# Masking attention scores in a state-space and feed-forward kernel: a select on GpSimd for one key block, four square matmul tiles for the other

## The chip, the core and the metric

The kernel runs on one core of a Trainium2 chip. A core has five engines with a queue of instructions each, worked off in order: TensorE (PE in the profile, its weight loads are PEld), VectorE (DVE), ScalarE (ACT), GpSimd (POOL) and SyncE (SP), which here only issues DMAs. Engines wait for one another by semaphores. TensorE writes its results to PSUM, eight banks of 128 partitions by 512 f32 numbers; the other tensors lie in SBUF.

The metric is the device time of the whole kernel in microseconds (us). The changed kernel is compared with the kernel before on the same chip.

## What is computed

32 sequences of 256 positions with 256 features go through a gated state-space layer, then through two transformer layers with local attention, and the input is added at the end. What the change touches is the local attention. The reference, cut to it:

```python
def local_attention(q, k, v):
    b, h, n, d = q.shape                  # n = 256 positions, 8 heads, d = 64
    w = n // WINDOW                       # WINDOW = 128: two windows
    bq = q.reshape(b, h, w, WINDOW, d) * QK_SCALE
    ...
    bk, bv = (look_around(bk), look_around(bv))   # the window before, and the own one
    ...
    sim = jnp.einsum('bhwid,bhwjd->bhwij', bq, bk)
    i = bt[:, :, None]
    j = btk[:, None, :]
    mask = (i < j) | (i > j + WINDOW) | (j == -1)
    sim = jnp.where(mask, -jnp.finfo(sim.dtype).max, sim)
    attn = jax.nn.softmax(sim, axis=-1)
    out = jnp.einsum('bhwij,bhwjd->bhwid', attn, bv)
    return out.reshape(b, h, n, d)

x = x + _L0_ffn_ref(_L0_cond_ref(x, cond_2048, ...), ...)
```

A query at position i sees the keys from i - 128 to i. With keys in two blocks of 128: the first block's keys are seen by queries of both windows (256 columns, of which a band is masked at either end), the second block's keys only by queries of the second window (128 columns, a triangle of which is masked).

## The kernel before

Sequences are worked in 4 groups of 8 (`NG`, `GB`). Two kinds of work run beside each other. The scan of the state-space layer takes a group at a time through 256 positions: for every position a row is loaded over 128 partitions (`xrep`, L675), scaled on ScalarE (L696), added with a clip on VectorE (`step`, L706, the tile `h`) and read out by TensorE (`read_out`, L718, the tile `y`). GpSimd takes part with the convolution's first tap (`acc`, L477) and the norms (L555, L576, L577).

Beside it run the two attention and feed-forward layers for the group whose scan is done. There are 64 pieces of this, one for each sequence and layer; the code calls the pair of group and layer `Attention(g, l)` and lists the pieces in `seqs`. Each piece is cut into stages, `ST = 8` per piece, and consecutive pieces overlap: `stage(n, i, what)` puts `what` into stage 8n + i, and the main loop calls all that stands in a stage, then lets the scan advance by its share. Within this order a scheduler may still move instructions past each other on an engine; what is wrapped in `tc.keep_in_program_order` stays where it is. The last group's pieces (`apart` is true) run when no scan is left.

`attend` sets the stages of a piece's attention: `project` makes queries, keys and values from the residual (L973) and rotates queries and keys (`rotated`: ScalarE L986, VectorE L989, L994, L999, L1003, GpSimd L997, L1005, L1006), `turn` transposes them (L1012) so that features lie on partitions, two heads above each other: head r of a pair on partitions 64r to 64r + 63.

`scores(b, kw, i0, n)` then works on key block `kw` (0 or 1) and `n` pairs of heads from `i0`. The result `sc` has keys on partitions and queries on columns, one bank per r, each with n parts of `nq` columns: 256 for the first block, 128 for the second. So the first block takes two calls with n = 2, the second one call with n = 4. Where `apart` is false, TensorE first writes the mask into the bank: a matmul of the identity with `mask_t` in bf16 (L1175), 0 where a key is seen and -32768 where it isn't. The score matmuls (L1182) add to that. Both operands have 64 partitions, so that two of them, one per r, fit above each other into the array (64*128 in the profile's rows). ScalarE takes the exponential into `pT` (L1191); -32768 becomes 0.

Where `apart` is true, there is no mask on TensorE: `start` is set on each score matmul, and `mask` (L1203) multiplies the exponentials by `mask_1` of 0 and 1, on GpSimd for the second key block and on VectorE for the first.

`sums` (stage 7) adds the exponentials over the keys on TensorE, four heads side by side as column tiles of 32 (L1212, 128*32 in the rows), and inverts the sum on VectorE (L1220). `values` (stage 7) multiplies with the values in two column tiles of 64 (L1231). The rest of the piece are the division (L1255), the output projection (L1023) and the feed-forward part: `normalise` with `rstd` (L1287), `apply` (L1295), `spread` (L1307), `widen` (L1335, `pa`), `product` (L1353, `ag`) and `narrow` (L1362, `po_f`).

All of PSUM is one pool of eight banks (`ps_w`), and `pT` has six buffers.

Of the kernel before, what the change touches and what calls it, by code (L numbers as in the profile page):

```python
# [14 lines left out]
ALU = mybir.AluOpType  # L15
# [23 lines left out]
W = 128  # L39
# [13 lines left out]
def bc(ap, axis, n):  # L53

    ap = ap.unsqueeze(axis)
    shape = list(ap.shape)
    shape[axis] = n
    return ap.broadcast_to(shape)
# [15 lines left out]
def kernel(  # L74
# [29 lines left out]
    nc = tc.nc  # L104
# [58 lines left out]
    for j in range(NJ):  # L163
# [18 lines left out]
        out=mask_t[:, 0:W], in_=mask_t[:, 0:W], compare_op=ALU.is_ge, fill=MASKED_LOW,  # L182
        base=0, pattern=[[1, W]], channel_multiplier=-1,
    )
    nc.gpsimd.affine_select(
        out=mask_t[:, W : 2 * W], in_=mask_t[:, W : 2 * W], compare_op=ALU.is_ge,
        fill=MASKED_LOW, base=0, pattern=[[-1, W]], channel_multiplier=1,
    )

    mask_1 = const.tile([P, 2 * W], BF, tag="mask_1", name="mask_1")  # L190
# [31 lines left out]
    def program(ctx, exact):  # L222
# [810 lines left out]
        if exact:  # L1033

            mask = rpool.tile([P, 2 * W], FP, tag="mask", name="mask")
            nc.gpsimd.memset(mask, 0.0)
            nc.gpsimd.affine_select(
                out=mask[:, 0:W], in_=mask[:, 0:W], compare_op=ALU.is_ge, fill=MASKED,
                base=0, pattern=[[1, W]], channel_multiplier=-1,
            )  # L1040
            nc.gpsimd.affine_select(
                out=mask[:, W : 2 * W], in_=mask[:, W : 2 * W], compare_op=ALU.is_ge, fill=MASKED,
                base=0, pattern=[[-1, W]], channel_multiplier=1,
            )
# [93 lines left out]
        class Attention:  # L1138
# [27 lines left out]
            def scores(self, b, kw, i0, n):  # L1166


                qT, kT, _ = self.qkv[b]
                nq = S - kw * W  # L1170
                banks = []
                for r in range(2):
                    sc = ps_w.tile([P, n, nq], FP, tag="w", name="sc")
                    if not self.apart:
                        nc.tensor.matmul(  # L1175
                            sc, ident_b, bc(mask_t[:, 0:nq], 1, n), start=True, stop=False
                        )
                    banks.append(sc)
                for i in range(n):
                    for r in range(2):  # L1180
                        rows = slice(r * DH, (r + 1) * DH)
                        nc.tensor.matmul(  # L1182
                            banks[r][:, i, :],
                            kT[rows, i0 + i, kw * W : (kw + 1) * W],
                            qT[rows, i0 + i, kw * W :],
                            start=self.apart,
                            stop=self.apart or i == n - 1,
                        )
                for r in range(2):
                    p = aw.tile([P, n, nq], FP, tag="pT", name="pT", bufs=6)  # L1190
                    nc.scalar.activation(p, banks[r], AF.Exp)  # L1191
                    self.ps[kw, i0, r] = p
                    for i in range(n):
                        self.p[b, kw, i0 + i, r] = p[:, i, :]

            def mask(self, kw, i0):

                e = nc.gpsimd if kw else nc.vector
                for r in range(2):
                    p = self.ps.pop((kw, i0, r))  # L1200
                    n, nq = p.shape[1:]
                    tc.keep_in_program_order(
                        e.tensor_mul(p, p, bc(mask_1[:, 0:nq], 1, n))  # L1203
                    )

            def sums(self, b):

# [207 lines left out]
        def stage(n, i, what, *args):  # L1415
            stages.setdefault(ST * n + i, []).append(partial(what, *args))

        def attend(n, at, b, nxt):

            stage(n, 0, at.turn, b, 1)  # L1420
            stage(n, 3, at.scores, b, 0, 0, 2)
            stage(n, 2, at.scores, b, 1, 0, HEADS // 2)
            stage(n, 5, at.scores, b, 0, 2, 2)
            if at.apart:
                for i, what in ((3, (1, 0)), (4, (0, 0)), (6, (0, 2))):
                    stage(n, i, at.mask, *what)
            stage(n, 7, at.sums, b)
            stage(n, 7, at.values, b)
            stage(n + 1, 0, at.put_inverse)
            stage(n + 1, 2, at.load_inverse)  # L1430
            stage(n + 1, 4, at.divide, b)
            stage(n + 1, 6, at.finish, b)
            if nxt is not None:
                for w in range(NW):
                    for i, a in ((0, 2), (1, 0), (1, 1)):
                        stage(n, 3 * w + i, nxt[0].project, nxt[1], w, a)
                stage(n, 6, nxt[0].turn, nxt[1], 0)
# [27 lines left out]
        for n, (g, l, b) in enumerate(seqs):  # L1465
            nxt = (ats[n + 1], seqs[n + 1][2]) if n + 1 < len(seqs) else None
            attend(n, ats[n], b, nxt)
            feed(n, g, l, b)
# [24 lines left out]
        for t in range(max(stages) + 1):  # L1493
# [3 lines left out]
            g, r = divmod(t + 1 + group - reload, group)  # L1497
# [124 lines left out]
```

## Time and profile before

| | us |
|---|---|
| median of 3 runs (3637.0 to 3640.93) | 3637.98 |
| the profiled execution's own time | 3633.24 |
| its span, first to last instruction | 3631.4 |
| busy in the span: TensorE | 3511.0 |
| VectorE | 2684.7 |
| ScalarE | 2160.2 |
| GpSimd | 1816.2 |
| L1175, mask matmuls: 288, busy | 88.1 |
| L1182, score matmuls of 256 columns: 1024 records, busy | 145.2 |
| L1182, score matmuls of 128 columns: 1024 records, busy | 74.4 |

The granted clock of TensorE was 0.990 over the span. The durations are those of the one profiled execution. A matmul with f32 operands stands twice in the records, so 1024 records are 512 matmuls. The row of a group gives the busy time of all its instructions together, with overlaps counted once, and then the mean duration of one; since matmuls overlap, the two differ.

The page's view in 40 slices shows how busy each engine is along the span, in tenths:

```profile
PE   7999989999999999999999999999999999999999
DVE  5888889878887877877787878777877545555553
ACT  3566656666666666666666666666666444544443
POOL 4433456545555455545555556455544454544551
```

In the first 5 or 6 slices the scan of the first group runs alone. From there to slice 32 scan and layers run beside each other; the last slices are the last group's layers.

### The profile page before, as it was taken

How to read it: one execution, taken by the hardware profiler on the slowest of the kernel's cores; microseconds unless marked ns; L12 is line 12 of the kernel's file. 1: busy time of each engine (PE TensorE's matmuls, PEld its weight loads, DVE VectorE, ACT ScalarE, POOL GpSimd, SP SyncE). 2: the span in 40 equal slices, each digit the busy share in tenths (PEclk: the TensorE clock that was granted, in tenths of full speed). 3: DMA queues.
4: the chain of work that ended last, by engine and by line, in shares of the span. 5: the costliest groups of instructions: out<-in, count | busy, mean ns of one | idle time of the engine just before them, and what ended most of it. 6: DMA issues, size and time to landing. Idle time of an engine off the chain costs nothing.

```text
span 3631.4 us, 56312 instructions
## 1 busy us (share of the span) xinstructions
PE 3511.0 (97%) x19548; PEld 2271.0 (63%) x19548; DVE 2684.7 (74%) x5113; ACT 2160.2 (59%) x3689; POOL 1816.2 (50%) x1746
## 2 busy tenths in 40 slices
PE   7999989999999999999999999999999999999999
PEld 4444335666666666666666666666666677777677
DVE  5888889878887877877787878777877545555553
ACT  3566656666666666666666666666666444544443
POOL 4433456545555455545555556455544454544551
PEclk9999999999999999999999999999999999999999
DMA  7877665545554555444454555534454112011111
GB/s 196 210 203 207 184 174 144 133 114 135 133 138 127 148 143 145 132 118 123 117 141 125 134 150 138 139 105 129 114 140 119 52 44 66 12 30 33 37 27 37
DMA packets 468763, 435.59 MB, mean 120 GB/s; under 512 B 228724, under 2 KB 308085, under 8 KB 468341
## 3 DMA queue, kind: packets, MB, share of 16 engines
q1 hardware_dynamic: 384018, 419.88, 42.5%
q10 hardware_dynamic: 84450, 12.01, 2.1%
q8 instruction: 158, 2.59, 0.3%
q14 instruction: 137, 1.11, 0.1%
HBM read 383.54 MB, written 46.66 MB: 118 GB/s over the span
## 4 chain that ended last, share of the span: by engine, by line
PE 62%; DVE 18%; DMA 7%; POOL 6%; ACT 4%; issue 3%; SPq 0%; ACTq 0%; DVEq 0%; POOLq 0%
PE ps_qkv L973 13%; PE pa L1335 12%; DVE h L706 7%; PE po_f L1362 7%; PE y L718 4%; DMA xrep<-xnd 4%; PE ps_wo L1023 4%; PE sc L1182 4%; PE ov L1231 3%; DVE acc L488 2%; PE ps_out L796 2%; PE tr_qk L1012 2%; PE ps_in L398 2%; ACT xrep L696 2%; PE rs L1212 2%
## 5 line engine op out<-in xcount | busy, mean ns | idle before, releaser
L706 DVE CUSTOM_DVE_ANT_0 h<-h,xrep,lim 128x512 f32<-128x512 f32 x1024 | 950.8, 928 | 226.5 <-ACT xrep L696 193.6
L696 ACT ACTIVATE xrep<-xrep,beta 128x512 f32<-128x512 f32 x960 | 673.2, 719 | 356.6 <-DMA xrep<-xnd 258.0
L973 PE MATMUL ps_qkv<-qkv,res 128*128 128x512 f32 x1536 | 715.0, 600 | 21.0 <-DVE ag L1353 9.7
L1335 PE MATMUL pa<-hT,w 128*128 128x256 f32 (+1 forms) x2816 | 679.9, 383 | 1.6 <-ACT hT L1313 0.9
L1335 PEld LDWEIGHTS pa<-hT,w 128*128 128x128 f32 (+1 forms) x2816 | 514.9, 188 | 147.5 <-issue 55.7
L997 POOL TENSOR_TENSOR rot<-rot,swp 128x512 f32<-128x512 f32 x256 | 336.1, 1313 | 441.3 <-DVE swp L994 330.8
L973 PEld LDWEIGHTS ps_qkv<-qkv,res 128*128 128x128 f32 x1536 | 280.1, 190 | 310.4 <-issue 239.7
L1005 POOL TENSOR_TENSOR rn<-ss,neg_half 128x8 f32<-128x8 f32 x256 | 459.3, 1794 | 18.0 <-DVE ss L1003 8.0
L718 PE MATMUL y<-h,ly 128*32 128x512 f32 x2048 | 361.7, 615 | 11.7 <-DVE h L706 9.3
L1287 POOL TENSOR_TENSOR rstd<-ve,neg_half 128x2 f32<-128x2 f32 x64 | 46.3, 723 | 609.6 <-DVE ve L1285 592.1
L1362 PE MATMUL po_f<-ag,w 128*128 128x256 f32 x1280 | 307.4, 387 | 5.1 <-DVE fo L1373 5.1
L1006 POOL TENSOR_TENSOR rot<-rot,rn 128x512 f32<-128x512 f32 x256 | 292.4, 1142 | 20.1
L1353 DVE SCALAR_TENSOR_TENSOR ag<-pa,b_sb,ag 128x256 f32<-128x256 f32 x320 | 152.7, 477 | 197.7 <-ACT ag L1346 197.3
L1362 PEld LDWEIGHTS po_f<-ag,w 128*128 128x128 f32 x1280 | 236.1, 191 | 69.4 <-issue 11.9
L986 ACT ACTIVATE sq<-ps_qkv 128x512 f32<-128x512 f32 x256 | 151.8, 595 | 208.3 <-PE ps_qkv L973 148.7
L1346 ACT ACTIVATE ag<-pa,b_sb 128x256 f32<-128x256 f32 x320 | 150.1, 469 | 177.3 <-PE pa L1335 175.2
L488 DVE SCALAR_TENSOR_TENSOR acc<-xr,wc_sb,acc 128x256 f32<-128x256 f32 x384 | 192.5, 526 | 56.7 <-POOL acc L477 55.4
L1023 PE MATMUL ps_wo<-oT,wo 128*128 128x256 f32 x1024 | 231.7, 379 | 1.4 <-ACT ag L1346 1.4
L989 DVE TENSOR_TENSOR rot<-ps_qkv,rc_sb 128x512 f32<-128x512 f32 x256 | 175.3, 685 | 75.8 <-ACT sq L986 75.7
L1182 PE MATMUL sc<-qT,kT 64*128 64x128 f32 (+1 forms) x2048 | 219.6, 343 | 0.0
L1191 ACT ACTIVATE pT<-sc 128x512 f32<-128x512 f32 x384 | 208.4, 596 | 12.6 <-PE sc L1182 10.5
L1023 PEld LDWEIGHTS ps_wo<-oT,wo 128*128 128x128 f32 x1024 | 194.3, 190 | 29.3 <-ACT ag L1346 2.2
(157 smaller groups left out, 5653.3 us busy)
## 6 DMA issues: line engine op xcount, KB each, us to landing
xrep<-xnd SPq DMA_DIRECT2D x960, 256.0 KB
rb<-inv SPq DMA_DIRECT2D x128, 256.0 KB
xnd<-xn SPq DMA_DIRECT2D x64, 256.0 KB
qkv<-in_wqkv_dram SPq DMA_DIRECT2D x24, 512.0 KB
ahead<-xs_a SPq DMA_DIRECT2D x48, 256.0 KB
xp<-ahead SPq DMA_DIRECT2D x48, 256.0 KB
xd<-xnd SPq DMA_DIRECT2D x192, 64.0 KB
w<-in_w_dram SPq DMA_DIRECT2D x80, 128.0 KB
```

The lines of the kernel that those rows point to most:

```text
L488: nc.vector.scalar_tensor_tensor(acc, xr[:, :, k : k + CH], wc_sb[:, ch, k : k + 1], acc, ALU.mult, ALU.add,)
L696: scaled = nc.scalar.activation(bx, ck[c].pop(("bx", t), bx), AF.Copy, scale=ck[c]["beta"][:, t : t + 1])
L706: nc.vector._custom_dve(TENSOR_ADD_SAT, out=h_new, in0=state["h"], in1=bx, s0=ck[c]["lim"][:, 0, t : t + 1], s1=ck[c]["lim"][:, 1, t : t + 1],
L718: nc.tensor.matmul(ck[c]["y", hb][32 * q : 32 * q + 32, :], ly[hb % 2][:, 32 * t : 32 * t + 32], ck[c].pop(("h", hb * TB + t)), start=(i = ...
L973: nc.tensor.matmul(ps, res[b][:, k, t0 : t0 + W], wt["qkv", a][:, k], start=(k == 0), stop=(k == KM - 1),)
L997: nc.gpsimd.tensor_add(rot, rot, swp)
L1005: nc.gpsimd.tensor_tensor(rn, ss, neg_half, ALU.pow)
L1006: nc.gpsimd.tensor_mul(rot, rot, bc(rn, 2, DH))
L1023: nc.tensor.matmul(po[:, d], wt["wo", 0][:, c, d * P : (d + 1) * P], oT[:, c, :], start=(c == 0), stop=(c == NC_ - 1),)
L1182: nc.tensor.matmul(banks[r][:, i, :], kT[rows, i0 + i, kw * W : (kw + 1) * W], qT[rows, i0 + i, kw * W :], start=self.apart, stop=self.apa ...
L1335: nc.tensor.matmul(dst[x], wt["w1", m][:, k, x], self.h[:, k], start=(k == 0), stop=(k == KM - 1),)
L1362: nc.tensor.matmul(self.po[:, d], wt["w2", 0][:, m, d * P : (d + 1) * P], self.ag[m], start=(m == 0), stop=(m == len(MCH) - 1),)
```

## The change

In the second key block (`kw` = 1) of all groups TensorE writes no mask any more. The exponentials of all entries are taken, and `mask` then runs in every piece: GpSimd's `affine_select` goes over `pT` and writes 0 wherever the column (the query) is less than the partition (the key). It reads one tensor, where the multiplication that the last group had before read two. `mask` for the second key block now stands in stage 3 for all pieces, one stage after its scores.

In the first key block of the groups 0 to 2 the mask matmuls stay. The score matmuls are cut in two by keys: keys 0 to 63 with the queries 0 to 191, keys 64 to 127 with the queries 64 to 255. Each is 64 partitions by 64 columns of weights and 192 columns long, and with two heads they lie on four square tiles of the array (row half by r, column half by keys). The queries left out for either half are masked for all of its keys, and hold what the mask matmul wrote.

The last group's first key block is as before, on VectorE.

```diff
@@ scores
                 nq = S - kw * W
+                masked = kw == 0 and not self.apart
+                nm = 2 if masked else 1
+                mk = W // nm
                 banks = []
                 for r in range(2):
                     sc = ps_w.tile([P, n, nq], FP, tag="w", name="sc")
-                    if not self.apart:
+                    if masked:
                         nc.tensor.matmul(
                             sc, ident_b, bc(mask_t[:, 0:nq], 1, n), start=True, stop=False
                         )
...
-                        nc.tensor.matmul(
-                            banks[r][:, i, :],
-                            kT[rows, i0 + i, kw * W : (kw + 1) * W],
-                            qT[rows, i0 + i, kw * W :],
-                            start=self.apart,
-                            stop=self.apart or i == n - 1,
-                        )
+                        for m in range(nm):
+
+                            k0 = m * mk
+                            q0, q1 = (k0, k0 + W + mk) if masked else (0, nq)
+                            nc.tensor.matmul(
+                                banks[r][k0 : k0 + mk, i, q0:q1],
+                                kT[rows, i0 + i, kw * W + k0 : kw * W + k0 + mk],
+                                qT[rows, i0 + i, kw * W + q0 : kw * W + q1],
+                                start=not masked,
+                                stop=not masked or i == n - 1,
+                            )
@@ mask
-                e = nc.gpsimd if kw else nc.vector
                 for r in range(2):
                     p = self.ps.pop((kw, i0, r))
                     n, nq = p.shape[1:]
-                    tc.keep_in_program_order(
-                        e.tensor_mul(p, p, bc(mask_1[:, 0:nq], 1, n))
-                    )
+                    if kw:
+                        masked = nc.gpsimd.affine_select(
+                            out=p, in_=p, compare_op=ALU.is_ge, fill=0.0, base=0,
+                            pattern=[[0, n], [1, W]], channel_multiplier=-1,
+                        )
+                    else:
+                        masked = nc.vector.tensor_mul(p, p, bc(mask_1[:, 0:nq], 1, n))
+                    tc.keep_in_program_order(masked)
@@ attend
             stage(n, 5, at.scores, b, 0, 2, 2)
+            stage(n, 3, at.mask, 1, 0)
             if at.apart:
-                for i, what in ((3, (1, 0)), (4, (0, 0)), (6, (0, 2))):
+                for i, what in ((4, (0, 0)), (6, (0, 2))):
                     stage(n, i, at.mask, *what)
```

## The prediction

> **What bounds the kernel now.** I read the page's busy shares first, then busy time by stage, then the chain of waits, then the rows of the instructions that change, and last the timeline of single score calls.
>
> The page's first part, and two stretches of the view of busy time by stage (each engine's busy us, with the count of its instructions):
>
> ```profile
> PE 3511.0 (97%) x19548; PEld 2271.0 (63%) x19548; DVE 2684.7 (74%) x5113; ACT 2160.2 (59%) x3689; POOL 1816.2 (50%) x1746
> ...
> 527.00:2960.00 2433.00, 2380.52 (x13842) 1561.02 (x13842) 1908.11 (x3599) 1544.17 (x2637) 1284.25 (x1192) 1.00 0.47 126
> 2960.00:3631.00 671.00, 663.55 (x3852) 480.62 (x3852) 346.01 (x689) 311.12 (x492) 305.23 (x244) 1.00 0.13 35
> ```
>
> TensorE leads in both. The stretch 527 to 2960 us holds the 48 sequences of the first three groups, whose scores get their mask from TensorE; there TensorE is busy 97.8%, VectorE 78%, GpSimd 53%. The last stretch holds the 16 sequences of the last group (`apart`). One sequence of the first kind takes 2433 / 48 = 50.7 us.
>
> Busy 97.8% doesn't mean that each us taken from TensorE is a us off the time. So next the chain of waits, first over the whole span, by engine, and then by line for 527 to 2960 us:
>
> ```profile
> PE 62%; DVE 18%; DMA 7%; POOL 6%; ACT 4%; issue 3%; SPq 0%; ACTq 0%; DVEq 0%; POOLq 0%
> ...
> by line: PE ps_qkv L973 11.9%; PE pa L1335 10.9%; DVE h L706 7.2%; PE po_f L1362 5.9%; PE y L718 4.2%; DMA xrep<-xnd 4.0%; PE ps_wo L1023 4.0%; PE sc L1182 3.6%; PE ps_out L796 3.2%; issue 3.2%; DVE acc L488 3.1%; PE ov L1231 3.1%; POOL rn
> ```
>
> TensorE holds 62% of the chain, not 97%. In between the chain leaves TensorE for VectorE's scan steps (`h`, L706), the loads of `xrep`, and GpSimd; TensorE works there too, but a shorter TensorE stretch only makes it wait sooner. The score matmuls (L1182) hold 3.6% of 2433 us = 88 us of the chain; their busy time in that stretch is 164.7 us by the same view of stages taken for that line. So about 53% of a saving in the scores is on the path.
>
> **What the Trainium skill says.** "Trainium Kernel Development and Optimization", section Quick Reference, calls matmul busy time a bad metric since matmuls are pipelined. The trace agrees: a mask matmul lasts 380 ns in its row, but its successor starts 0.21 us after it (below). "TensorEngine Tiling (Array Packing)", section Key Properties, says that tiles work in parallel and that a change of the tiling mode drains the engine; both can be seen below. "TensorE: Matmul & The Clock Gate", section Measured speedup vs the span model, has 16 tiles by row and column at 10.6 times; the trace of before shows row halves (L1182) and column tiles (L1212, L1231) side by side, but never both at once. "GPSIMD Engine Reference", section Engine selection, says that two-input work is about twice as slow on GpSimd as on VectorE and one-input work is near line rate; the trace agrees in kind (rows below).
>
> The timeline of TensorE around one score call of the first key block, with the second mask matmul from a narrower window, and the rows of what is exchanged (mean ns after the busy us):
>
> ```profile
> 1429.17 0.59 PE L1175 MATMUL sc<-mask_t,ident_b 128*128 128x512 bf16 x2
> ...
> 1429.38 0.38 PE L1175 MATMUL sc<-mask_t,ident_b 128*128 128x512 bf16 x1
> ...
> 1429.69 1.13 PE L1182 MATMUL sc<-qT,kT 64*128 64x256 f32 x8
> 1430.76 1.06 PE L718 MATMUL y<-h,ly 128*32 128x512 f32 x8
> ...
> L1203 POOL TENSOR_TENSOR pT<-pT,mask 128x512 f32<-128x512 f32 x32 | 36.3, 1155 | 1.8 <-ACT pT L1191 1.8
> L290 POOL COPY wide<-wx_sb 128x512 f32<-128x512 f32 x3 | 2.0, 674 | 0.0
> L185 POOL TENSOR_SCALAR_AFFINE_SELECT mask_t<-mask_t 128x128 bf16<-128x128 bf16 x1 | 0.3, 292 | 0.0
> ```
>
> Read the starts. First mask to second: 0.21 us for 512 bf16 columns. Second mask to first score: 0.31, so some 0.10 goes to the change from the full array to row halves. Eight score records (each f32 matmul is recorded twice) take 1.07 us from 1429.69 to 1430.76. They go in pairs, one per row half, and the start of the second pair is 0.32 after the first, the third and fourth 0.21 to 0.22 after the one before: a pair of 256 columns streams in 0.215 us, and the first also shows 0.10 of weight load that nothing hides. The rest to `y` is the drain.
>
> **The change part by part.**
> *Second key block, groups 0 to 2.* Two mask matmuls per sequence go, 48 x 2 = 96. The mode change before the scores stays, since what stands ahead is mostly full array work. So 96 x 0.215 = 21 us of TensorE work. Ends: 0.19 per pair if the change cost grew, 0.52 if the mode change went too; 9 to 25 us.
> *First key block, groups 0 to 2.* Two calls per sequence, 96 in all. The mask matmuls stay. Of 4 matmuls of 256 columns on two row halves become 8 of 192 columns on four square tiles; the 64 columns left out are fully masked ones, and they keep the large negative value that the mask matmul put there. If four tiles run at once, a step costs 0.215 x 192/256 = 0.16 us and the call has four steps as before: 4 x 0.215 + 0.10 = 0.96 before, 4 x 0.16 + 0.05 = 0.69 after. (The 0.05 is my estimate for the unhidden load of 64 weights, half of that of 128.) 0.27 x 96 = 26 us. If the column halves don't overlap: 8 steps of 0.16 + 0.05 = 1.33, or +0.37 x 96 = +36 us. I take the first: the denominator row `rs` (L1212) runs four column tiles so, 32 records in 1.44 us from start to start of the next line on the timeline.
> *Sum on TensorE:* 21 + 26 = 47 us of work less. The order of TensorE's instructions shows few other moves (about 400 lines of 7800 differ, most of them these), and changes of tiling mode fall from 1196 to 1182. On the path 53% of 47: 25 us.
> *GpSimd.* 96 new selects in groups 0 to 2, and in the last group 32 selects in place of 32 multiplications at 1155 ns. A select of 512 f32 elements isn't in the trace. From below, the one-input copy of that size, 674 ns; from above, four times the 128-element select, 4 x 292 = 1168. I take 0.9, since the fixed part of a short one counts four times in the upper end. New work 96 x 0.9 = 86 us in a stretch where GpSimd has 1149 us idle. The select waits for ScalarE's exponentials, and as GpSimd works in order, what stands behind it waits too: by the order, mostly the rotation (L997, L1005, L1006), also `acc` (L477) and `xn` (L576). VectorE waits for `acc` and for `rstd`, TensorE's transposes for `rot`. GpSimd has 6% of the chain, 218 of its 1816 busy us or 12%; at that share the selects cost 86 x 0.12 = 10 us. Ends: 0, as it sits in idle time, and 86 x 0.38 = 33, if every select delays it in the 38% of the time in which the chain is off TensorE.
> The sums of the exponentials come at stage 7, the select at stage 3, so 4/8 of 50.7 us lie between: no wait there. VectorE and ScalarE keep their work; a two-input step `h` may be held up by GpSimd's reads (its durations run from 707 to 1866 ns); with one input to read I take nothing for it, up to 10 us.
> *Last group.* TensorE is 98.9% busy there and its work is the same; GpSimd's 32 x 0.25 = 8 us less is hidden by TensorE: 0.
> *Sum:* 25 - 10 = 15 us off. Against the profiled execution's 3633.2 (span 3631.4 and 1.8 around it): 3618. The median of the runs shown lies 4.8 above that: 3623.
>
> **Rivals.**
> *All of TensorE's saving counts.* For it: 97.8% busy, and its named waits in that stretch are small (the largest, for a free bank after L1353, 10.3 us in all). Against: the chain has 38% elsewhere. 47 less some 5 for GpSimd: 3596.
> *The saving is hidden.* What is taken from TensorE comes back as waits for `h` and `xrep`, because VectorE's bursts set the pace of each sequence, and the path share at the margin falls quickly. About 25 x 0.4 - 10 = 0: 3638, give or take 7.
> *Slower: GpSimd's queue.* A select that is issued before its exponentials are done stands at the head of the queue and holds up `rn` and `rot` of the next sequence's keys, and `acc` of the scan. It decides when a pair of selects costs the path over 25 / 48 = 0.5 us per sequence; with the upper end of 33 and 3 for waits at the head it's 36 - 25 = 11 us: 3649. For it: GpSimd's `rn`, `rot` and `acc` are on the chain. Against: its longest waits are idle time before `rstd` and L997.
> *The tiles don't do what they say* (column halves in turn): TensorE +36 - 21 = +15, of it 53% = 8, and 10 for GpSimd: 3656. Against: the column tiles of L1212.
>
> **How the numbers follow.** Forecast 0.46 (its own range 3610 to 3633), full saving 0.20, hidden 0.16, GpSimd's queue 0.14, tiles in turn 0.04. No change means within 0.2%, 7.3 us, about what a measurement of this kernel can tell. Faster: 0.20 and nearly all of 0.46, 0.63; the same: 0.16 and 0.03; slower: 0.18. The range goes down to the full saving with its upper ends, 3592, and up to where half of the slower cases lie, 3647.
>
> **What would show it.** Mask matmuls 192 instead of 288; score records of 64 x 192 that start in fours some 7 ns apart, fours 0.16 us apart, and a call of 0.8 us; a select row of 0.7 to 1.2 us, x128. Idle time of TensorE in the first three groups up from 52 us to some 85 (47 us of work less, 15 us of time), and their stretch some 15 us shorter, the last group's 671 us the same. Fours further apart than 0.2 us would speak for the tiles in turn; waits of `rn`, `acc` or `rot` behind the select on the chain for GpSimd's queue. I am wrong if the share of the scores on the chain isn't what a saving there is worth.

## The result and the profile after

The changed kernel takes 3622.39 us (median of 5 runs, 3616.12 to 3624.52), the kernel before 3637.98 beside it: the medians are 16 us apart, and the ratio is 0.995, with a 95% interval of 0.9936 to 0.9963. Measured once more beside other kernels it had 0.9961 (0.9953 to 0.9969, from 17 runs). The two ratios are 18 and 14 us less; below, the gain is taken as 14 to 18 us. The forecast was 3623.

First the page's busy shares, its chain by engine, and busy time by stage for the first three groups and for the last, of the changed kernel:

```profile
PE 3476.2 (96%) x20220; PEld 2251.9 (62%) x20220; DVE 2687.0 (74%) x5113; ACT 2157.7 (60%) x3689; POOL 1897.4 (52%) x1842
...
PE 58%; DVE 20%; POOL 7%; DMA 6%; ACT 5%; issue 3%; SPq 0%; ACTq 0%; DVEq 0%; POOLq 0%
...
527.00:2945.00 2418.00, 2339.48 (x14459) 1536.01 (x14459) 1915.18 (x3598) 1542.48 (x2638) 1379.20 (x1287) 0.99 0.48 127
2945.00:3622.00 677.00, 670.02 (x3912) 485.84 (x3910) 342.02 (x692) 313.14 (x496) 290.75 (x246) 1.00 0.13 35
```

TensorE's share of the chain falls from 62% to 58%, VectorE's and GpSimd's rise: what was taken from TensorE isn't all on the path. TensorE idles 2418 - 2339 = 79 us in the first stretch, 52 before. GpSimd has 81 us more to do.

The instructions that changed, from the groups by form, and TensorE's timeline around one score call of the first key block:

```profile
L1209 POOL TENSOR_SCALAR_AFFINE_SELECT pT<-pT 128x512 f32<-128x512 f32 x128 | 99.2, 791 | 1.8 <-ACT pT L1198 1.8
L1189 PE MATMUL sc<-qT,kT 64*64 64x192 f32 x1536 | 87.3, 342 | 0.0
...
L1178 PE MATMUL sc<-mask_t,ident_b 128*128 128x512 bf16 x192 | 59.7, 381 | 20.3 <-DVE ag L1364 19.5 <-DVE zT L787 0.4 <-DVE swp L994 0.4
```

```profile
1415.93 0.59 PE L1178 MATMUL sc<-mask_t,ident_b 128*128 128x512 bf16 x2
1416.45 0.88 PE L1189 MATMUL sc<-qT,kT 64*64 64x192 f32 x16
1417.27 0.70 PE L973 MATMUL ps_qkv<-qkv,res 128*128 128x512 f32 x1
```

From start to start the call takes 1417.27 - 1416.45 = 0.82 us, where it took 1.07. The single records in the trace start in fours, 6 to 7 ns apart, and the fours are 0.21, 0.16 and 0.16 us apart. One pass of 192 columns takes 0.16 us, and four matmuls start within 20 ns: so four square tiles do run at once. The select lasts 0.79 us on average (median 0.64), and GpSimd stood still for its exponentials only 1.8 us in all: it isn't issued too early.

Where along the span the gain comes can be read off the start of the first denominator matmul (`rs`) of each piece in the records. In us, against before; piece 48 is the first of the last group. Each row is one execution, and "again" is a second one of the changed kernel, so differences of some 5 us are scatter: up to piece 0 nearly the same work runs in all of them, and still that column goes from -6.5 to +3.4:

```
piece              0      8     16     24     32     40     48     60
before, us     553.1  963.5 1390.2 1803.9 2218.7 2632.6 2997.7 3468.8
after           -1.4   -0.1   +1.1   +0.8   +2.0   -2.4   -8.5   -8.5
after, again    -2.4   -1.1   -2.3   -3.9   -2.5   -7.3  -13.5  -13.5
tiles only      -1.4   -2.1   -4.6   -6.1   -5.7   -9.8  -13.3  -13.3
no select       -6.5   -7.3  -12.3  -19.3  -25.3  -32.5  -39.4  -39.4
select twice    +3.4   +9.1  +13.1  +13.9  +20.8  +19.2  +14.0  +14.0
```

From piece 48 on nothing changes, as forecast: TensorE paces the last group and has the same work. But the changed kernel gains next to nothing in its first 32 pieces. (The profiled execution is the slowest of the five; its total is 9 us less.) This didn't look like a gain that is spread evenly. It raised a second theory, the scan theory: that a us of TensorE is worth nothing while the scan runs beside it, and all of it once the scan thins out. The path-share theory below is the prediction's: a us of TensorE is worth 0.53 everywhere in groups 0 to 2.

### The profile page after: what moved, and what is told of

It is laid out like the page before. It is cut to its first block, busy times and chain, and to the rows that moved or that the text cites. A ratio compares the mean times of both kernels' runs of the same rounds, so it can differ in the third digit from the quotient of the medians.

```text
span 3622.8 us, 57709 instructions
## 1 busy us (share of the span) xinstructions
PE 3476.2 (96%) x20220; PEld 2251.9 (62%) x20220; DVE 2687.0 (74%) x5113; ACT 2157.7 (60%) x3689; POOL 1897.4 (52%) x1842
## 4 chain that ended last, share of the span: by engine, by line
PE 58%; DVE 20%; POOL 7%; DMA 6%; ACT 5%; issue 3%; SPq 0%; ACTq 0%; DVEq 0%; POOLq 0%
PE pa L1346 12%; PE ps_qkv L973 12%; DVE h L706 7%; PE po_f L1373 6%; DMA xrep<-xnd 5%; PE ps_wo L1023 4%; PE y L718 4%; PE ov L1242 3%; PE sc L1189 3%; DVE acc L488 3%; PE ps_out L796 2%; ACT xrep L696 2%; PE tr_qk L1012 2%; POOL acc L477 2%; POOL rn L1005 2%
## 5 line engine op out<-in xcount | busy, mean ns | idle before, releaser
L488 DVE SCALAR_TENSOR_TENSOR acc<-xr,wc_sb,acc 128x256 f32<-128x256 f32 x384 | 195.4, 537 | 61.8 <-POOL acc L477 60.5
L1189 PEld LDWEIGHTS sc<-qT,kT 64*64 64x64 f32 (+1 forms) x2816 | 134.5, 158 | 115.1 <-issue 89.5
```

What stands on the lines that cost most here:

```text
L488: nc.vector.scalar_tensor_tensor(acc, xr[:, :, k : k + CH], wc_sb[:, ch, k : k + 1], acc, ALU.mult, ALU.add,)
L1189: nc.tensor.matmul(banks[r][k0 : k0 + mk, i, q0:q1], kT[rows, i0 + i, kw * W + k0 : kw * W + k0 + mk], qT[rows, i0 + i, kw * W + q0 : kw * ...
```

## The experiments

All ratios are to the kernel before on the same chip, with their 95% interval; 0.1% is 3.6 us.

**The parts alone, without the select, and with twice the select**

The tiles alone keep the second key block's mask matmul in groups 0 to 2:

```diff
-                masked = kw == 0 and not self.apart
-                nm = 2 if masked else 1
+                masked = not self.apart
+                nm = 2 if masked and kw == 0 else 1
...
-            stage(n, 3, at.mask, 1, 0)
             if at.apart:
+                stage(n, 3, at.mask, 1, 0)
```

> The first key block's four square tiles alone; the second block's mask stays on TensorE in groups 0 to 2 (the select is left to the last group). 26 us of TensorE work less, no work added on GpSimd. Path-share theory (each us of TensorE in groups 0 to 2 is worth 0.53): 14 us faster than before, spread evenly over the 48 pieces. Scan theory (a us of TensorE is worth nothing while the scan paces the pieces, and all of it only in about the last 12 of the 48 pieces): 6 to 7 us faster, with pieces 0 to 32 at the same times as before.

Measured: 0.9972 (0.9965 to 0.9979), 10 us faster. In the table above the gain grows from the first pieces on, which speaks against the scan theory's "pieces 0 to 32 at the same times"; at piece 32 it is hardly more than the scatter, and the kernel without select, below, decides it.

The select alone:

```diff
-                nm = 2 if masked else 1
+                nm = 1
```

> The second key block's select alone; the first block's scores on two row halves as before. 21 us of TensorE work less, 96 selects of some 0.78 us on GpSimd. Path-share theory: 11 us less for TensorE, 9 us more for GpSimd: 2 us faster, no change that can be told. Scan theory with a select that costs nothing: 5 us faster, gained in the last 12 of the 48 pieces.

Measured: 1.003 (1.0018 to 1.0042), 11 us slower. Neither theory had it so: the select must cost more than TensorE gains by losing the mask.

Without mask and select in the second key block of groups 0 to 2, and with each select issued twice:

```diff
-            stage(n, 3, at.mask, 1, 0)
             if at.apart:
+                stage(n, 3, at.mask, 1, 0)
```

```diff
                     tc.keep_in_program_order(masked)
+                    if kw and not self.apart:
+                        tc.keep_in_program_order(nc.gpsimd.affine_select(
+                            out=p, in_=p, compare_op=ALU.is_ge, fill=0.0, base=0,
+                            pattern=[[0, n], [1, W]], channel_multiplier=-1,
+                        ))
```

> The changed kernel with the second key block's masking left out in groups 0 to 2: neither mask matmul nor select, so masked keys count in the sums there. TensorE work as in the changed kernel, GpSimd work as before. Path-share theory: 9 us faster than the changed kernel, 25 us faster than before. Scan theory: the same as the changed kernel within 3 us if the selects sit in idle time; if it is faster by 8 or more and pieces 0 to 32 gain, it was the selects that ate the gain there.

> The changed kernel with each select of groups 0 to 2 issued twice in a row (the second changes nothing). 96 more GpSimd instructions of some 0.78 us, 75 us in all. Path-share theory: 9 us slower than the changed kernel. Scan theory with idle GpSimd: the same as the changed kernel within 3 us. If GpSimd's queue paces the pieces: 30 us or more slower.

Measured: 0.9906 (0.9893 to 0.992) without, 34 us faster than before; 1.0036 (1.0023 to 1.005) with two, 13 us slower. So the first 96 selects cost 0.995 - 0.9906 = 0.44% to 0.9961 - 0.9906 = 0.55%, 16 to 20 us, and the second 96 cost 0.75 to 0.86%, 27 to 31 us. That is 0.2 to 0.3 us of path for a select of 0.79 us, with GpSimd busy only 52%. In the table the run without select has gained 25 us by piece 32, where the changed kernel has gained nothing: the scan theory falls, and it was the selects that ate the gain there.

Part of this cost came as a lower clock of TensorE. Its granted clock, the mean over the runs, was 0.988 without select, 0.987 in the changed kernel and 0.983 with twice the select; beside each, the kernel before had 0.989. From 0.988 to 0.983 is 0.5% of 3600 us, some 18 us if all of it counted (an estimate). How a select gets there is seen further down.

**How a select costs**

First the changed kernel once more, for comparison on the same chip:

> The changed kernel once more, so that the other runs of this set can be compared with it on the same chip. 0.995 of the time before, within 0.002. Its gain by pieces: if it is again near 0 in pieces 0 to 32 and comes after, it is the change's and not the one execution's.

Measured: 0.9961 (0.9953 to 0.9969). The row "after, again" has the same shape as the first.

There are two ways in which a select could cost. As GpSimd works in order, it can hold up what stands behind it. Or, since it reads and writes SBUF, it can hold up VectorE beside it. A power of two numbers per partition occupies GpSimd about as long but moves almost nothing. Its result goes to a scratch tile that nothing reads, so the second key block's masking is left out there in groups 0 to 2:

```diff
+    scr = const.tile([P, NJ], FP, tag="scr", name="scr")
...
-                    if kw:
+                    if kw and not self.apart:
+                        masked = nc.gpsimd.tensor_tensor(scr, p[:, 0, 0:NJ], half, ALU.pow)
+                    elif kw:
                         masked = nc.gpsimd.affine_select(
```

> The changed kernel with each select of groups 0 to 2 replaced by a power of 128x2 numbers, which reads two of the exponentials and writes a scratch tile: the same place in GpSimd's queue, some 0.73 us instead of 0.78, but almost nothing moved to or from SBUF. The second key block's masking is left out in those groups. Queue theory (a select costs by holding up what is behind it on GpSimd): about the time of the changed kernel, 16 to 20 us slower than without select. Access theory (a select costs by holding up VectorE's two-input instructions, above all the scan step, beside it): the time of the kernel without select, 16 to 20 us faster than the changed kernel.

Measured: 0.9931 (0.9916 to 0.9946), between the two: 9 us slower than without select, 11 faster than the changed kernel beside it. The row of the power says that it stays on GpSimd even longer than a select:

```profile
L1210 POOL TENSOR_TENSOR scr<-pT,half 128x2 f32<-128x2 f32 x96 | 92.9, 968 | 2.2
```

So the place on GpSimd alone doesn't explain the cost. In the records TensorE and ScalarE have exactly the same order of instructions in both kernels, VectorE's differs at 26 places of 5113, TensorE nowhere waits for a select in stage 3, and the granted clock is 0.987 in both. What is left for the 11 us is the access to SBUF. It can be seen directly. The changed kernel's timeline of GpSimd and VectorE around two selects:

```profile
1263.28 1.67 POOL L1209 TENSOR_SCALAR_AFFINE_SELECT pT<-pT 128x512 f32<-128x512 f32 x2
1263.39 1.06 DVE L706 CUSTOM_DVE_ANT_0 h<-h,xrep,lim 128x512 f32<-128x512 f32 x1 [0.18 <-ACT xrep L696]
```

The scan step starts 0.12 us after the first select and lasts 1.06 us, where a step with nothing beside it takes some 0.80. In the records the first select ends at 1263.91, the step 0.54 us after it, and the second select stretches to 1.09 us. This repeats: of the 28 steps that start inside a select in the records, 25 end 0.52 to 0.56 us after it ends. VectorE seems to do most of such a step only when the select is through, and a select issued during a step waits for that step. All 1024 steps together, in the changed kernel and with the power:

```profile
L706 DVE CUSTOM_DVE_ANT_0 h<-h,xrep,lim 128x512 f32<-128x512 f32 x1024 | 956.7, 934 | 217.6 <-ACT xrep L696 186.1
```

```profile
L707 DVE CUSTOM_DVE_ANT_0 h<-h,xrep,lim 128x512 f32<-128x512 f32 x1024 | 946.1, 924 | 220.7 <-ACT xrep L697 189.3 <-DVE h L707 7.2 <-PE y L719 1.9
```

That is 10 us of VectorE's time. It isn't shown that all of it is on the path. Nor is the power quite free of such delays: most of its 96 take either some 0.70 us or 1.14 and more.

The other thing is where the select stands. Two runs move it, one to stage 5, one to stage 6; a third moves the power to stage 5:

```diff
-            stage(n, 3, at.mask, 1, 0)
+            stage(n, 3 if at.apart else 5, at.mask, 1, 0)
```

> The changed kernel with the select of groups 0 to 2 in stage 5 instead of stage 3. The same work at another place of GpSimd's queue, mostly behind the second half of the rotation instead of inside it. Queue theory: up to 15 us faster than the changed kernel, as the rotation isn't held up, unless what stands behind it now (acc, the norms) is as pressing. Access theory: within 5 us of the changed kernel, by how much of the scan lies beside it.

> The changed kernel with the select of groups 0 to 2 in stage 6, one stage before the sums that need it. If place in GpSimd's queue is what matters: between stage 3 (ratio 0.996) and stage 5 (0.9937), since by the order the selects stand ahead of the rotation again. If it is only how late it stands: as stage 5 or better, unless the sums begin to wait.

> The power of 128x2 numbers in place of the select, in stage 5: queue time without access to SBUF, at the better place; the second key block's masking is left out in groups 0 to 2. If stage 5 takes the queue part away: the ratio of the kernel without select, 0.990 to 0.991, and what the select in stage 5 costs above that is access. If it still costs as much as in stage 3: 0.993.

Measured: stage 5 0.9937 (0.9921 to 0.9952), 9 us faster than the changed kernel beside it; stage 6 0.9965 (0.9957 to 0.9973), like stage 3; the power in stage 5 0.9892 (0.9877 to 0.9907), which costs nothing against the kernel without select. So stage 5 takes away the cost of the place. That stage 6 loses what stage 5 gains doesn't mean that later is worse: in GpSimd's order 72 of the 96 selects stand at the same place of the rotation in stage 6 as in stage 3, and 41 in stage 5, where the others stand behind more of it.

In stage 5 the select is still 0.9937 - 0.9892 = 0.45%, 16 us, slower than the power. That isn't all access, since the sums need the select's result and nothing needs the power's. In stage 5 TensorE waits for it, as it did in no piece of stage 3:

```profile
PE rs L1223 <- POOL pT L1209: 8.6, 16, 1.2
```

That leaves some 7 us of the 16 for access and for what else differs, which isn't separated.

What the place costs shows on TensorE as well. The view of waits for 527 to 2960 us has the mask matmuls of the first key block waiting for a bank that VectorE's `ag` frees (us in total, times, longest). In the changed kernel, with the power in stage 3, without select, with the select in stage 5, and with the power in stage 5:

```profile
PE sc L1178 <- DVE ag L1364: 19.5, 13, 2.2
```

```profile
PE sc L1179 <- DVE ag L1367: 19.3, 13, 2.2
```

```profile
PE sc L1178 <- DVE ag L1364: 5.6, 7, 0.8
```

```profile
PE sc L1178 <- DVE ag L1364: 5.6, 7, 0.9
```

```profile
PE sc L1179 <- DVE ag L1367: 5.7, 7, 0.9
```

Stage 3 costs 14 us of waits there, whatever the instruction is, and stage 5 none; stage 6 has 20.0 us, like stage 3. In two places on the timeline, `ag` stands on VectorE behind several `acc` of the convolution (L488), some of which wait for GpSimd's `acc`. VectorE's waits for that `acc` are 37.0 us in all without select, 47.5 in the changed kernel, 53.4 with the power in stage 3, and 39.5 and 42.0 with the two in stage 5. The order of instructions on TensorE, VectorE and ScalarE is the same in stages 3, 5 and 6, from first to last. So it is GpSimd's queue that makes these 14 us.

The clock falls after some of these waits. In the changed kernel TensorE waited six times over 2.1 us for `ag`, and within 1.3 us of the end of three of these waits its granted clock was half for 3.4 us. One of them, where the score call takes 1.55 us instead of 0.88:

```profile
2001.35 0.38 PE L1178 MATMUL sc<-mask_t,ident_b 128*128 128x512 bf16 x1 [2.11 <-DVE ag L1364]
2001.65 1.55 PE L1189 MATMUL sc<-qT,kT 64*64 64x192 f32 x16
```

With twice the select these waits grow to 3.5 us, and the records have 14 such stretches between 527 us and piece 48, 4 without select. Why the clock falls, no run here tests.

**What a microsecond of TensorE is worth**

The mask matmuls of the second key block left out of the kernel before, and issued twice in it:

```diff
-                    if not self.apart:
+                    masked = kw == 0 and not self.apart
+                    if masked:
                         nc.tensor.matmul(
                             sc, ident_b, bc(mask_t[:, 0:nq], 1, n), start=True, stop=False
                         )
...
-                            start=self.apart,
-                            stop=self.apart or i == n - 1,
+                            start=not masked,
+                            stop=not masked or i == n - 1,
```

```diff
+                        if kw:
+                            nc.tensor.matmul(
+                                sc, ident_b, bc(mask_t[:, 0:nq], 1, n), start=False, stop=False
+                            )
```

> The kernel before with the second key block's mask matmuls left out in groups 0 to 2 and nothing in their place; the first block on two row halves as before. TensorE 21 us less, nothing added. If a us of TensorE is worth 0.72 whatever part it comes from: 15 us faster than before. If the parts add up (tiles alone gave 11, both without select gave 34): 23 us faster, more than the mask matmuls last. At 0.53: 11 us.

> The kernel before with the second key block's two mask matmuls issued twice in groups 0 to 2: 96 more mask matmuls, 21 us of TensorE work more, the output the same. It asks what a us of TensorE is worth when added. At the path share of 0.53: 11 us slower than before. At 0.72: 15 us slower. If TensorE had slack there: under 4 us.

Measured: 0.9965 (0.9952 to 0.9977) without, 13 us faster; 1.0046 (1.0032 to 1.006) with twice as many, 17 us slower. For 21 us of matmuls that is 0.6 and 0.8. The tiles have 10 us for 26, 0.4; both parts without select 34 for 47, 0.7. None of them is 0, and only the interval of the added masks reaches 1; it depends on where the saving stands. The two parts add up to 23 us, 11 less than both together have. The intervals are 3 to 5 us to either side, so the excess is somewhat larger than chance would make it. Its cause stays open; one difference is that the parts' kernels have another order of instructions on every engine (VectorE's differs from the changed kernel's at some 700 of 5113 places).

**A faster version**

In the last group TensorE is busy 99%, so a saving should count in full there. Four square tiles can be used there too, though without mask matmul the corners that no tile writes must be set to 0. On top of the select in stage 5:

```diff
-                nm = 2 if masked else 1
+                nm = 2 if kw == 0 else 1
...
-                    nc.scalar.activation(p, banks[r], AF.Exp)
+                    if self.apart and kw == 0:
+                        for m in range(nm):
+                            ks, qs = slice(m * mk, m * mk + mk), slice(m * mk, m * mk + W + mk)
+                            nc.scalar.activation(p[ks, :, qs], banks[r][ks, :, qs], AF.Exp)
+                        nc.gpsimd.memset(p[0:mk, :, W + mk :], 0.0)
+                        nc.gpsimd.memset(p[mk:, :, 0:mk], 0.0)
+                    else:
+                        nc.scalar.activation(p, banks[r], AF.Exp)
```

> The kernel with the select in stage 5, and the four square tiles in the last group's first key block too, where there is no mask matmul: the exponentials are then taken and multiplied as before by halves of the keys (the corners that no tile writes are set to 0 by GpSimd, the multiplication covers all of it). 32 calls of 0.27 us less TensorE work where TensorE is 98.9% busy: 8 to 9 us faster than with the select in stage 5 alone, so some 31 us faster than before, ratio 0.991; all of it after piece 48. If ScalarE's two half exponentials came late there, less or nothing.

Measured: 0.9921 (0.9908 to 0.9935), 29 us faster than before, and 6 us more than the select in stage 5 has, with intervals that overlap. The last group by stage, from the start of its first denominators to the end, with the select in stage 5 and then with the tiles as well:

```profile
2981.00:3615.00 634.00, 626.19 (x3658) 453.79 (x3657) 319.72 (x648) 292.47 (x463) 268.58 (x227) 1.00 0.13 34
```

```profile
2978.00:3604.00 626.00, 618.72 (x3899) 448.63 (x3897) 322.99 (x649) 316.30 (x523) 307.73 (x348) 1.00 0.13 35
```

The stretch is 8 us shorter, of 8 to 9 expected, and TensorE is busy 7.5 us less: here a us of TensorE is about a us of time. ScalarE's and GpSimd's additions, 24 and 39 us, are hidden. This is the fastest of the kernels that compute everything.

## Why the prediction was right, and where its terms were off

The total, 15 us off, came out at 14 to 18. Two of its terms were off by about as much, in opposite directions.

- *TensorE's work.* Mask matmuls fell from 288 to 192, as said. The call of the first key block fell by 0.25 us, 0.27 was forecast; fours 0.16 us apart. The rival of tiles in turn was wrong.
- *53% of it on the path, 25 us.* Mis-sized: 34 us with nothing added on GpSimd, 0.73 of the 47. Single parts had 0.39 to 0.80. The chain's share was a fair guide to the size, not a law. The full saving, the first rival, is out for groups 0 to 2; it would have been right for the last group.
- *The select's duration.* 0.9 was taken; 0.79 measured, 0.64 the median. The two-input multiplication that it replaces in the last group took 1155 ns on GpSimd before, and the one on VectorE 822: 1.4 times, not about twice.
- *10 us for GpSimd's queue.* The power in the select's place cost 9 us. The size was right, and so was `acc` as one of the ways; that it could be got rid of two stages later wasn't seen.
- *Nothing for VectorE's steps, "up to 10 us".* This is the term that failed. Access cost some 11 us in stage 3, as much as the queue; the intervals leave some 6 us to either side. One-input work on GpSimd was taken to leave VectorE alone. So the select cost 16 to 20 us, not 10. That the clock of TensorE falls a little with the select was in no term either.
- *GpSimd's queue as the slower rival* decides from 25 us on by the forecast's sum. The select alone shows that it was near: with the mask's saving and no tiles, the kernel is 11 us slower than before, and 24 us slower than with the mask simply left out.
- *Idle time of TensorE in the first three groups* was to rise to some 85 us: 79. Last group: from piece 48 to the end 633.7 us before, 633.6 after.

Had the path share been 0.5 and the select what it turned out to be, there would have been 5 us left; the 9 us too few for TensorE and the 6 to 10 too few for the select covered each other up.

## What to carry to other kernels

When an engine with half its time idle takes over work from a busy one, price its access as well as its queue: run the same place with an instruction that moves almost nothing, and the two come apart, as long as no engine waits for the result. The share of the chain is a usable price for a us of the busiest engine, within a factor of 1.5, and it isn't the same in each stretch; look for a stretch where the engine is alone: in the last group here it was about 1. And where such a helper instruction stands is worth a try at two or three places, since one stage was worth 9 us here and the next one nothing; look at the order that comes out, not at the stage's number.

## What the runs showed of the hardware

- Four f32 matmuls of 64 partitions by 64 columns start within 20 ns on the four quarters of the array, and four of 192 columns take 0.16 us a pass. Row halves and column halves work at once.
- A one-input select of 128x512 f32 on GpSimd takes 0.63 us at least, about 1.09 when VectorE's step gets in between, and 25 of 28 VectorE steps that start inside it end 0.54 us after it. A power on 128x2 numbers lasts 0.97 us on average in stage 3.
- After waits of 2.1 us of TensorE, three of six times in the changed kernel, its granted clock was half for 3.4 us; 16 score records then took 1.55 us instead of 0.88.
